# A network's first layer: the next gates issued tile by tile between turning steps, and one value through the gates' function behind each square root

## The chip, the cores and the metric

The kernel runs on one core of a Trainium2 chip. The metric is the device time of one execution in microseconds (us). Engines are named as in the profile: PE is TensorE's matmul, PEld its weight load, DVE is VectorE, ACT is ScalarE, POOL is GpSimd, SP is SyncE, which here only issues transfers (DMAs).

## The reference

The input is a batch of eight images of 56 x 56 pixels with 192 channels. Four layers follow one another, each behind a group normalization, with a residual sum. The change touches the first layer only:

```python
p = silu(x @ p_w.T + p_b);  q = silu(x @ q_w.T + q_b);  v = silu(x @ v_w.T + v_b)   # 192 -> 576
qv = q * v
o1 = toeplitz(qv along each row,    a1)    # a1, a2: 56 taps each way, per channel
o2 = toeplitz(qv along each column, a2)
out = (p * (o1 + o2)) @ o_w.T + o_b        # 576 -> 192
```

Layer 1 is a 3 x 3 outlook attention, layer 2 an 8 x 8 window attention with rotary positions, layer 3 a scan over rows and columns. All arithmetic is float32.

## The kernel before

**Stages of the first layer.** For each image `b` there are five stages `c` = 0 to 4. A stage handles 128 of the 576 channels; the fifth, the tail, has 64. A stage consists of four kinds of work:

- *Gates* (`project`): for four groups `g` of the image's pixels, `q` and `v` are computed, each by six matmul calls into one tile of PSUM (L358), then Silu with bias on ACT (L369) into an SBUF tile `s`. So a group has two PSUM tiles; in the tail it has one, whose two halves are `q` and `v`. The products (`multiply`, L381 on DVE and L387 on POOL) write `q * v` into `qv`, once straight and once transposed.
- *Turning* (`turn_both`, `turn`): PE transposes `qv` in seven steps of 16 transposes each (L414). A step fills one PSUM tile, which DVE copies into `ol` (L419), and after it ACT copies the other half into `or` (L419 too). The tail's steps are those of L433 and L440.
- *Convolution* (`convolve`): 32 matmul calls a step (L457), whose results DVE and ACT copy into `ot` (L477, L475, L468).
- *Post* (`post`, `post_tail`): the gate `p` (L499 or L612, Silu L506 or L618), the way back by transposes (L518 or L627, product on DVE L523 or L632), the output's matmuls (L532, L553, L640, L655), and the addition into the accumulator `acc` on DVE (L484, L486). Post of stages 0 and 1 runs in stage 2, that of 2 and 3 in stage 4, and that of the tail (`post_tail`) in stage 0 of the next image.

**One stage ahead.** In stage `c` the gates of stage `c + 1` are issued. The products of the next stage overwrite `qv`, so they come behind the turning steps. The gates need not: `early` holds the first two of the four groups, which are issued between turning steps, with their products directly behind the turning. The other two run behind that, as wholes.

```python
early = [] if fill else ahead[0:2]
ring["wide"] = c not in (2, 4)
merge(fill + [f for f, _ in early], turns)
```

`fill` is the post work that a stage takes over. It is present in stages 2 and 4, and in stage 0 of every image but the first. So gates go between turning steps in stages 1 and 3, and in stage 0 of image 0. `merge(a, b)` spreads the two lists evenly over each other.

**Buffers.** PSUM tiles come from a ring: three tiles `c` and, as every fourth where `ring["wide"]` holds, one tile `o`. A PE step that takes a tile waits until its earlier contents have been read by the engines that copy or add them. The SBUF tiles `s` are a ring of six.

**Normalization.** The statistics (`bn_stats`, L156 on DVE, twelve for the next image's input `x` and eleven for `acc`) and two small rounds of matmuls (L129) end in a square root on ACT (L170). In stage 0 the statistics of the finished `acc` are told to the next layer (`tell`), `acc` is stored (L71), and the next image's `x` is loaded (`load_raw`, L89, sixteen transfers into one of two buffers). In stage 1 `acc` is loaded anew (L73) and `tell` ends (L693). In stage 2 the next image is normalized (`normalize`, L49 and L680).

**Who orders what.** Only PE's instructions keep the order in which the program issues them (`manual_schedule` names PE alone for this layer). DVE's, ACT's, POOL's and SP's instructions are put into an order by the scheduler when the kernel is built. On the chip each engine then works its queue in that order, and an instruction whose input is not there holds up all behind it. SP has at most eight transfers under way: each one waits for the one eight places before it.

**Function tables.** Where ACT goes from Sqrt to Silu or back, a table load (ACT_TABLE_LOAD) stands in front of the activation.

Of the kernel before, what the change touches and what calls it, by code (L numbers as in the profile page):

```python
# [9 lines left out]
AF = mybir.ActivationFunctionType  # L10
# [37 lines left out]
def affine(eng, out, in_, scale, bias):  # L48
    eng.tensor_scalar(out, in_, scale, bias, ALU.mult, ALU.add)  # L49
# [128 lines left out]
def layer0(cx, xin, xout, w, consts):  # L178
# [6 lines left out]
    tc, nc = cx.tc, cx.nc  # L185
    B = len(xin)
    NS, DS = 9, 64
# [3 lines left out]
    halves = slice(0, CB), slice(CB, 128)  # L191
    cx.open(B)
    cx.between = ExitStack()
    with ExitStack() as es:
        gn = GroupNormSplit(cx, cx.between, w["gmat"], es, w["gmat3"])
# [8 lines left out]
        def banks():  # L204
            if ring["wide"]:
                ring["at"] += 1
                if ring["at"] % 4 == 0:
                    return cx.tile(psc, [128, 2, 512], "o", bufs=1)
            return cx.tile(psc, [128, 2, 512], "c")

        def work(*shape):
            n = int(np.prod(shape))
            t = cx.tile(wk, [128, 4 * 4 * H], "s")[:, 0:n]
            return t.rearrange("p (a b) -> p a b", a=shape[0])
# [10 lines left out]
        wqv, wps = {}, {}  # L225

        def fetch_wqv(q, queue=nc.sync):
            if q < B * NC:
                wqv[q] = cx.tile(cp, [128, 3, 2, 128], "wqv", bufs=2)
                queue.dma_start(wqv[q], w["w_qv"][q % NC])  # L230
# [12 lines left out]
        with ExitStack() as pes:  # L243
# [11 lines left out]
            n = 1  # L255
# [10 lines left out]
            for t in (1, 2):  # L266
# [13 lines left out]
                for i in range(3):  # L280
                    ps = banks()[0:32, 0, 0:NP]
# [4 lines left out]
                for s in range(NS):  # L286
                    ps = banks()[0:DS, 0, 0:NP]
# [54 lines left out]
        def project(xn, q):  # L342


            n = 7 * H
            c = q % NC
            tail = c == NC - 1
            js = [2 * c] if tail else [2 * c, 2 * c + 1]

            state = {}  # L350

            def gates(g):
                pss = []
                for i in range(len(js)):
                    ps = banks()
                    for k in range(3):
                        for h, rows in enumerate(halves):
                            nc.tensor.matmul(  # L358
                                ps[:, h, 0:n], wqv[q][rows, k, i, :],
                                xn[rows, k, g * n : (g + 1) * n],  # L360
                                start=(k == 0), stop=(k == 2),
                            )
                    pss.append(ps)
                ts = []
                for i in range(2):
                    j, ps = js[0 if tail else i], pss[0 if tail else i]
                    rows = slice(i * DS, (i + 1) * DS) if tail else slice(0, 128)
                    t = work(2, n)[0 : DS if tail else 128]
                    nc.scalar.activation(t, ps[rows, :, 0:n], AF.Silu, bias=bqv[rows, j : j + 1])  # L369
                    ts.append(t)  # L370
                state[g] = ts

            def products(g):
                multiply(g, slice(0, DS if tail else 128), state.pop(g))

            return [(lambda g=g: gates(g), lambda g=g: products(g)) for g in range(4)]

        def multiply(g, rows, ts):

            def straight():  # L380
                nc.vector.tensor_tensor(  # L381
                    sub(qv[rows, 7 * g :, 64 + H - 1 :], (HH * 120, 2), (120, 7), (-1, H)),
                    *(t.rearrange("p u (h w) -> p u h w", w=H) for t in ts), ALU.mult,
                )

            def across(eng, u, w0, w1):
                eng.tensor_tensor(  # L387
                    sub(qv[rows, w0:, H - 1 - 7 * g - HH * u :], (120, w1 - w0), (-1, 7)),
                    *(t[:, u].rearrange("p (h w) -> p w h", w=H)[:, w0:w1] for t in ts), ALU.mult,
                )  # L390

            if g < 3:
                straight()
                for u in range(2):
                    across(nc.gpsimd, u, 0, H)
                return

            for i, w in enumerate(((0, HH), (HH, H))):
                across(nc.gpsimd, 0, *w)
                across(nc.vector, 1, *w)  # L400
                if i == 0:
                    straight()
# [193 lines left out]
        def post_tail(xn, ot, acc):  # L596
# [68 lines left out]
            steps = [lambda f=f, g=g: f(g) for f in (back, out) for g in range(2)]  # L665
            return [gates, *steps, lambda: (rest(0), rest(1))]

        def normalize(xn):

            measures, deviate, settle = gn.steps(*((xn[:, k], 4) for k in range(3)))  # L670

            def measure():
                for f in measures:
                    f()

            def last():
                rstd, nbias = settle(banks)
                for k in (0, 2):
                    affine(nc.vector, xn[:, k], xn[:, k], rstd[:, k : k + 1], nbias[:, k : k + 1])
                nc.scalar.activation(  # L680
                    xn[:, 1], xn[:, 1], AF.Identity, bias=nbias[:, 1:2], scale=rstd[:, 1:2]
                )

            return [measure, lambda: deviate(banks), last]

        def tell(b, xa, xb):

            measures, deviate, settle = gn.steps((xa, 7), (xb, 4))

            def last(bank):  # L690
                nn = cx.tile(gn.small, [128, 2, 2], "nn")
                for i, v in enumerate(settle(bank)):
                    nc.vector.tensor_copy(nn[:, :, i], v)  # L693
                nc.sync.dma_start(cx.norms[b][0:CA], nn[:, 0, :])
                nc.sync.dma_start(cx.norms[b][CA:], nn[0:CB, 1, :])

            return measures, [deviate, last]

        def merge(a, b):

            n = max(len(a), len(b))
            for i in range(n):
                for x in (a, b):
                    for f in x[-(-i * len(x) // n) : -(-(i + 1) * len(x) // n)]:
                        f()
# [7 lines left out]
        xn, nxt = first, None  # L713
# [1 line left out]
        for n in range(2):  # L715
            toeplitz(n)
        def whole(steps):
            return [lambda f=f, h=h: (f(), h()) for f, h in steps]

        merge(whole(project(xn, 0)), [])  # L720
        fill, after, telling = [], None, []
        for b in range(B):
            more = b + 1 < B
            for c in range(NC):
                n = b * NS + 2 * c
                two = c < NC - 1
                turns = turn_both(n) if two else turn(n)

                i = b * NC + c
                fetch_wqv(i + 2)  # L730
                ahead = project(xn if two else nxt, i + 1) if two or more else []
                early = [] if fill else ahead[0:2]
                ring["wide"] = c not in (2, 4)
                merge(fill + [f for f, _ in early], turns)
                ring.update(at=0, wide=True)
                for _, f in early:
                    f()
                ahead = whole(ahead[len(early) :])
                if fill:
                    fetch_wp({2: 1, 4: 2, 0: 0}[c])  # L740
                fill, beside = [], []
                if c == 0:
                    if after is not None:
                        image_dma(nc.sync, xout[b - 1], *after, store=True)
                        beside, telling = tell(b - 1, *after)
                    if more:
                        nxt = load_raw(b + 1)
                if c == 1:
                    acc = new_acc(b)
                    beside = [lambda f=f: f(banks) for f in telling]  # L750
                if c == 2 and more:
                    beside = normalize(nxt)

                if c % 2 == 0:
                    ot = cx.tile(cp, [120, H, 128] if two else [H, H, DS], "ot")
                convs = []
                for m in (n, n + 1) if two else (n,):
                    *some, last = convolve(m, ot)
                    convs += some + [lambda m=m, last=last: (last(), toeplitz(m + 2))]

                if c == NC - 2:
                    k = len(ahead)
                    ahead = [f for pair in zip(ahead, convs[0:k]) for f in pair]
                    convs = convs[k:]
                merge(ahead, beside)
                for f in convs:
                    f()
                if c in (1, 3):
                    fill = post(c // 2, xn, ot, acc)
            fill, after = post_tail(xn, ot, acc), acc  # L770
            xn = nxt
# [1448 lines left out]
```

## Time and profile before

| | us |
|---|---|
| median of 3 runs | 4054.93 (4053.79 to 4061.73) |
| the profiled execution | 4069.0, of which the span is 4067.2 |
| PE busy in the span | 3786.1 (93%) |
| DVE / ACT / POOL busy | 2371.5 / 1789.6 / 1523.3 |
| first layer, from the first matmul to the last image's post | about 27 to 1935 |
| image 5, stage 0: from the tail's first post matmul to the first whole gates | 1231.0 to 1250.2 |

The rows read as follows. The page gives each engine's busy time. A row of the timeline gives start, duration, engine, line, operation and tiles, how many instructions are merged in it, and in brackets how long the engine had been idle before it and who ended that. A row of the windows gives, for one stretch, the busy time of PE, PEld, DVE, ACT and POOL with their counts, the granted clock, the DMA engines' share and their GB/s.

### The profile page before, as it was taken

To read this page: it belongs to the slowest core of one execution; us is meant where nothing else is said; L and a number is where in the kernel's file an instruction comes from. 1 tells how busy PE (TensorE), PEld (TensorE's weight loads), DVE (VectorE), ACT (ScalarE), POOL (GpSimd) and SP (SyncE) were. 2 spreads that over 40 slices of the span, in tenths; PEclk is the share of its full clock that TensorE was granted. 3 is DMA by queue.
4 is the path that set the end of the run, shared out by engine and by line. 5 is a ranking of instruction groups with operands and counts; after the bars stand their busy time and mean duration, and the time that the engine had idled before them with its cause. 6 is when DMAs were issued, how large, how long until landed. Compare 5 with 4: busy or idle time off the path is not lost. (4 is left out here: it accounts for less than half of the span.)

```text
span 4067.2 us, 115859 instructions
## 1 busy us (share of the span) xinstructions
PE 3786.1 (93%) x51036; PEld 2655.7 (65%) x51036; DVE 2371.5 (58%) x3318; ACT 1789.6 (44%) x2021; POOL 1523.3 (37%) x1325
## 2 busy tenths in 40 slices
PE   6989999999998999999799999899989999998997
PEld 4777767677776767777566666444435455556997
DVE  6556565655657565555544444565566667665654
ACT  2434444344444434443334433243335555554564
POOL 3222242222233222223433333333334444444776
PEclk9999999999999999999899999999999999999999
DMA  7865353533526352342333443556557766653333
GB/s 158 169 143 131 81 142 103 125 77 98 125 76 160 85 136 72 89 105 76 108 104 103 107 104 94 167 166 209 166 163 184 181 153 154 153 132 102 99 99 98
DMA packets 390300, 507.94 MB, mean 125 GB/s; under 512 B 176932, under 2 KB 326724, under 8 KB 388404
## 3 DMA queue, kind: packets, MB, share of 16 engines
q1 hardware_dynamic: 385621, 494.07, 47.6%
q8 instruction: 401, 6.57, 0.7%
q10 hardware_dynamic: 3135, 3.47, 0.3%
q0 software_dynamic: 1040, 2.99, 0.3%
q14 instruction: 103, 0.84, 0.1%
HBM read 344.69 MB, written 155.65 MB: 123 GB/s over the span
## 5 line engine op out<-in xcount | busy, mean ns | idle before, releaser
L387 POOL TENSOR_TENSOR qv<-s,s 128x392 f32<-128x392 f32 (+3 forms) x320 | 569.3, 1806 | 1296.4 <-ACT s L369 1048.5
L358 PE MATMUL c<-x,wqv 64*128 64x392 f32 x2856 | 518.3, 509 | 45.9 <-ACT or L419 24.7
L358 PEld LDWEIGHTS c<-x,wqv 64*128 64x128 f32 x2856 | 285.0, 193 | 223.6 <-ACT or L419 29.8
L369 ACT ACTIVATE s<-c,bqv 128x784 f32<-128x784 f32 (+1 forms) x270 | 244.9, 913 | 330.0 <-PE c L358 308.1
L381 DVE TENSOR_TENSOR qv<-s,s 128x784 f32<-128x784 f32 (+1 forms) x160 | 229.0, 1441 | 132.0 <-ACT s L369 132.0
L499 PE MATMUL c<-x,wp 64*128 64x224 f32 x2688 | 282.1, 356 | 17.0 <-ACT s L506 14.4
L419 DVE COPY ol<-c 56x1024 f32<-56x1024 f32 x184 | 218.7, 1208 | 113.6 <-PE c L414 113.6
L499 PEld LDWEIGHTS c<-x,wp 64*128 64x128 f32 x2688 | 254.5, 189 | 21.7 <-ACT s L506 16.6
L523 DVE TENSOR_TENSOR s<-s,c 128x896 f32<-128x896 f32 x112 | 121.8, 1088 | 239.6 <-ACT s L506 233.3
L419 ACT COPY or<-c 56x1024 f32<-56x1024 f32 x184 | 184.0, 1008 | 175.8 <-DVE ol L419 169.5
L457 PEld LDWEIGHTS c<-or,ol 120*64 120x64 f32 x7168 | 217.3, 139 | 40.4 <-issue 38.0
L457 PE MATMUL c<-or,ol 120*64 120x56 f32 x7168 | 225.3, 224 | 19.3 <-issue 10.1
L2084 POOL TENSOR_TENSOR y<-y,s 128x448 f32<-128x448 f32 x168 | 185.2, 1102 | 95.8 <-ACT s L2063 95.8
L1552 ACT ACTIVATE vb<-sm 128x1024 f32<-128x1024 f32 (+1 forms) x100 | 103.9, 1040 | 261.1 <-issue 218.2
L2053 PE MATMUL h<-ringv,am 128*64 128x57 f32 (+1 forms) x4400 | 192.7, 235 | 21.8 <-DVE ringv L2040 13.9
L506 ACT ACTIVATE s<-c,bp 128x448 f32<-128x448 f32 x224 | 129.7, 630 | 185.5 <-PE c L499 184.1
L1541 PE MATMUL v<-wvb,wa 128*128 128x512 f32 (+1 forms) x400 | 192.1, 613 | 6.4 <-ACT wa L1427 6.4
L2053 PE MATMUL h<-ringh,am 128*64 128x57 f32 (+1 forms) x4400 | 186.3, 232 | 8.8 <-DVE ringh L2059 8.8
L2053 PEld LDWEIGHTS h<-ringv,am 128*64 128x64 f32 x4400 | 168.1, 140 | 25.4 <-DVE ringv L2040 14.9
L1060 PE MATMUL c<-wv,xc 128*126 128x192 f32 x896 | 175.4, 339 | 0.0
L2053 PEld LDWEIGHTS h<-ringh,am 128*64 128x64 f32 x4400 | 166.3, 139 | 11.1 <-DVE ringh L2059 11.1
L1570 POOL TENSOR_TENSOR l<-vb,ta 128x512 f32<-128x512 f32 (+1 forms) x52 | 75.2, 1446 | 259.5 <-ACT vb L1552 258.5
(268 smaller groups left out, 7708.7 us busy)
## 6 DMA issues: line engine op xcount, KB each, us to landing
or<-tt SPq DMA_DIRECT2D x252, 196.0 KB
ol<-tt SPq DMA_DIRECT2D x252, 196.0 KB
vt<-v SPq DMA_DIRECT2D x56, 672.0 KB
v<-vb SPq DMA_DIRECT2D x96, 384.0 KB
x<-x SPq DMA_DIRECT2D x110, 168.0 KB
wqv<-in_l_w_qv SPq DMA_DIRECT2D x38, 384.0 KB
x<-in_x SPq DMA_DIRECT2D x64, 196.0 KB
x<-x SPq DMA_DIRECT2D x110, 112.0 KB
```

Source lines behind the costliest of these rows:

```text
L358: nc.tensor.matmul(ps[:, h, 0:n], wqv[q][rows, k, i, :], xn[rows, k, g * n : (g + 1) * n], start=(k == 0), stop=(k == 2),)
L369: nc.scalar.activation(t, ps[rows, :, 0:n], AF.Silu, bias=bqv[rows, j : j + 1])
L381: nc.vector.tensor_tensor(sub(qv[rows, 7 * g :, 64 + H - 1 :], (HH * 120, 2), (120, 7), (-1, H)), *(t.rearrange("p u (h w) -> p u h w", w= ...
L387: eng.tensor_tensor(sub(qv[rows, w0:, H - 1 - 7 * g - HH * u :], (120, w1 - w0), (-1, 7)), *(t[:, u].rearrange("p (h w) -> p w h", w=H)[:, ...
L419: copy(dst[:, :, :, i0 : i0 + 8], view[rows])
L457: nc.tensor.matmul(ps[u * 64 : (u + 1) * 64, k, v * H : (v + 1) * H], left[:, d * H : d * H + 64], right[:, d * H : (d + 1) * H], start=Tr ...
L499: nc.tensor.matmul(ps[:, h, u * n : (u + 1) * n], wps[j][rows, k, u, :], xn[rows, k, g * n : (g + 1) * n], start=(u == 0 and k == 0), stop ...
L506: nc.scalar.activation(sp[:, u].rearrange("p (h i) -> p h i", h=2), ps[:, :, u * n : (u + 1) * n], AF.Silu, bias=bp[:, 2 * j + u : 2 * j + ...
L1060: nc.tensor.matmul(out(i, u), group(i, u), wv[0], start=(u == 0), stop=True, skip_group_check=True,)
L1541: nc.tensor.matmul(out, x[:, at : at + n], wt, start=(k == 0), stop=(k == 1), skip_group_check=True,)
L2053: nc.tensor.matmul(ps[sides[c], y], am[a][:, m * CB : (m + 1) * CB], old[:, x], start=(n < 2), stop=True, skip_group_check=True,)
L2084: nc.gpsimd.tensor_tensor(v, v, line[:, j], ALU.add)
```

## The change

Four edits, all in the first layer.

1. `gates(g)`, which issued both PSUM tiles of a group and then both activations, becomes `gate(g, i)` for one tile and its activation. `project` returns for each group a list of such calls and the products.
2. `early` is filled in stages 0, 1 and 3 of every image. So stage 0 of images 1 to 7, the stage that carries the tail's post, gets the first two groups too.
3. The tile calls are first spread over `fill`, and the result over the turning steps. In stage 0 this gives ten pieces (six of post, four gate tiles) over seven turning steps; in stage 1 four gate tiles.
4. `ready()` puts a single value through Silu, into a tile that nothing reads. It is called behind both square roots, in the last image only where a gate follows.

```diff
-            def gates(g):
-                pss = []
-                for i in range(len(js)):
-                    ps = banks()
...
-                    pss.append(ps)
-                ts = []
-                for i in range(2):
-                    j, ps = js[0 if tail else i], pss[0 if tail else i]
-                    rows = slice(i * DS, (i + 1) * DS) if tail else slice(0, 128)
+            def gate(g, i):
+                ps = banks()
...
+                j = js[i]
+                for rows in halves if tail else [slice(0, 128)]:
                     t = work(2, n)[0 : DS if tail else 128]
                     nc.scalar.activation(t, ps[rows, :, 0:n], AF.Silu, bias=bqv[rows, j : j + 1])
-                    ts.append(t)
-                state[g] = ts
+                    state.setdefault(g, []).append(t)
...
-            return [(lambda g=g: gates(g), lambda g=g: products(g)) for g in range(4)]
+            return [
+                ([lambda g=g, i=i: gate(g, i) for i in range(len(js))], lambda g=g: products(g))
+                for g in range(4)
+            ]
...
+        def ready():
+            t = cx.tile(gn.small, [1, 1], "ready")
+            nc.scalar.activation(t, gn.eps[0:1], AF.Silu)
...
                 rstd, nbias = settle(banks)
+                ready()
...
-                for i, v in enumerate(settle(bank)):
+                told = settle(bank)
+                if b + 1 < B:
+                    ready()
+                for i, v in enumerate(told):
...
-            return [lambda f=f, h=h: (f(), h()) for f, h in steps]
+            return [lambda fs=fs, h=h: [f() for f in (*fs, h)] for fs, h in steps]
...
-                early = [] if fill else ahead[0:2]
+                early = ahead[0:2] if c in (0, 1, 3) else []
                 ring["wide"] = c not in (2, 4)
-                merge(fill + [f for f, _ in early], turns)
+                woven = []
+                merge(
+                    [lambda f=f: woven.append(f) for f in fill],
+                    [lambda f=f: woven.append(f) for fs, _ in early for f in fs],
+                )
+                merge(woven, turns)
```

More of the change, by code (lines that the diff above doesn't have):

```diff
@@ L350, in project @@
             state = {}
-            def gates(g):
-                pss = []
-                for i in range(len(js)):
-                    ps = banks()
[L356 to L362, printed above, removed]
-                    pss.append(ps)
-                ts = []
-                for i in range(2):
-                    j, ps = js[0 if tail else i], pss[0 if tail else i]
-                    rows = slice(i * DS, (i + 1) * DS) if tail else slice(0, 128)
+            def gate(g, i):
+                ps = banks()
+                for k in range(3):
+                    for h, rows in enumerate(halves):
+                        nc.tensor.matmul(
+                            ps[:, h, 0:n], wqv[q][rows, k, i, :],
+                            xn[rows, k, g * n : (g + 1) * n],
+                            start=(k == 0), stop=(k == 2),
+                        )
+                j = js[i]
+                for rows in halves if tail else [slice(0, 128)]:
                     t = work(2, n)[0 : DS if tail else 128]
                     nc.scalar.activation(t, ps[rows, :, 0:n], AF.Silu, bias=bqv[rows, j : j + 1])
-                    ts.append(t)
-                state[g] = ts
+                    state.setdefault(g, []).append(t)
             def products(g):
                 multiply(g, slice(0, DS if tail else 128), state.pop(g))
-            return [(lambda g=g: gates(g), lambda g=g: products(g)) for g in range(4)]
+            return [
+                ([lambda g=g, i=i: gate(g, i) for i in range(len(js))], lambda g=g: products(g))
+                for g in range(4)
+            ]
         def multiply(g, rows, ts):
@@ L731, in layer0 @@
                 ahead = project(xn if two else nxt, i + 1) if two or more else []
-                early = [] if fill else ahead[0:2]
+                early = ahead[0:2] if c in (0, 1, 3) else []
                 ring["wide"] = c not in (2, 4)
-                merge(fill + [f for f, _ in early], turns)
+                woven = []
+                merge(
+                    [lambda f=f: woven.append(f) for f in fill],
+                    [lambda f=f: woven.append(f) for fs, _ in early for f in fs],
+                )
+                merge(woven, turns)
                 ring.update(at=0, wide=True)
```

## The prediction, made before the changed kernel ran

> **What bounds the kernel now.** I read the page first: engines, then groups.
>
> ```profile
> span 4067.2 us, 115859 instructions
> ...
> PE 3786.1 (93%) x51036; PEld 2655.7 (65%) x51036; DVE 2371.5 (58%) x3318; ACT 1789.6 (44%) x2021; POOL 1523.3 (37%) x1325
> ...
> L419 DVE COPY ol<-c 56x1024 f32<-56x1024 f32 x184 | 218.7, 1208 | 113.6 <-PE c L414 113.6
> ```
>
> PE is the bound on the whole, so the time is PE's work plus the idle time of PE, and a stretch in the first layer is worth what PE gains or loses in it. Next I cut stage 0 of image 5 into windows: the turning with the tail's post, then the four whole groups of gates, then the convolution.
>
> ```profile
> 1231.00:1250.20 19.20, 14.72 (x226) 9.21 (x222) 16.82 (x25) 8.64 (x9) 0.07 (x1) 1.00 0.79 205
> 1250.20:1266.30 16.10, 16.10 (x96) 9.21 (x96) 16.03 (x28) 8.41 (x9) 9.47 (x6) 1.00 0.90 216
> 1266.30:1276.80 10.50, 7.80 (x258) 7.63 (x256) 7.48 (x11) 1.82 (x2) 3.30 (x3) 1.00 1.02 236
> ```
>
> In the turning window PE works 14.72 of 19.20 us, but DVE works 16.82. In the gates' window PE is full. PE's timeline says where the 4.5 us of idle time are.
>
> ```profile
> 1240.16 0.93 PE L640 MATMUL c<-s,wo 64*128 64x392 f32 x4 [0.77 <-ACT or L419]
> ...
> 1242.18 1.59 PE L640 MATMUL c<-s,wo 64*128 64x392 f32 x8 [0.61 <-ACT or L419]
> ...
> 1245.20 0.89 PE L655 MATMUL o<-s,wo 64*64 64x392 f32 x8 [0.97 <-ACT or L419]
> ...
> 1248.75 0.68 PE L414 MATMUL c<-ident,qv 64*120 64x64 f32 x16 [1.38 <-ACT or L419]
> 1250.17 1.26 PE L358 MATMUL c<-x,wqv 64*128 64x392 f32 x6 [0.74 <-PE c L414]
> ```
>
> Each wait is for a PSUM tile that DVE and, after DVE, ACT must empty ("ACT or L419" starts when DVE's `ol` has ended). Images 1 to 7 show the same five waits (0.77, 0.61, 0.97, 1.38, 0.74). Stage 1 has one, 1.86 us, before its first whole gates. DVE's timeline gives the prices and the order of its queue:
>
> ```profile
> 1238.99 0.95 DVE L632 TENSOR_TENSOR s<-s,o 128x784 f32<-128x784 f32 x1
> ...
> 1241.01 1.97 DVE L486 TENSOR_TENSOR acca<-c,acca 128x392 f32<-128x392 f32 x4
> ...
> 1249.99 2.33 DVE L419 COPY ol<-c 56x1024 f32<-56x1024 f32 x2
> 1252.26 2.71 DVE L156 BATCH_NORM_STATS2 st<-acca 128x6 f32<-128x448 f32 x5
> ...
> 1260.07 1.96 DVE L156 BATCH_NORM_STATS2 st<-x 128x6 f32<-128x392 f32 x4
> ```
>
> The statistics of the next `x` (the last row, st<-x) stand 10 us behind the last turning copy (1249.99 plus 2.33).
>
> **Part 1: gate tiles into stage 0 (images 1 to 7).** Four gate tiles of 2.04 us (24 matmuls in 8.2 us) move from the gates' window into the turning window. On PE alone this would fill the 4.5 us. But DVE's order is the scheduler's, and the program as built shows it. Copies of steps 0 to 6 are t0 to t6, way back is B, two additions to `acc` are "+", statistics of `acc` and `x` are a and x, the straight product is Q, the aggregate is g:
>
> ```
> before: t0 B t1 B t2 + + t3 + a + t4 (accb+) a (accb+) t5 t6 | a a a a a ... x x ...
> after:  t0 t1 B t2 x x x x B t3 + x + t4 Q a a x + a + t5 a a a a x g x x t6 Q (accb+) (accb+) ...
> ```
>
> Nine of the next image's twelve `x` statistics, five more of `acc`'s, and one product now stand in front of the seventh copy, t6. That matters twice. First, the wait: the four x in front of the second B need two halves of `x` that SP issues at 1235.7 to 1239. In the old trace the landing events put the fifth of these transfers (needed by the first x) at 1244.44, 13.4 us into the stage; in images 1 to 6 at 12.6 to 13.5. The seventh, which the third x needs, I put at 14.5, by the 0.5 us between landings. DVE gets there at 10.5: PE gives t0, t1, B, t2 by 8.4, and t2's copy ends at 10.5. So DVE, and behind it the second B, every later copy and addition, stands for 3 us. Second, the work behind the wait, by the distances of the rows above: four x 1.96, B 0.88, four copies (t3 to t6) at 1.16 make 4.64, eight additions at 0.49 make 3.94, five x at 0.49 make 2.45, seven a at 0.54 make 3.79, Q 0.95, g 0.22. Together 18.8, so t6's copy ends at 13.5 + 18.8 = 32.3, and ACT's half at 33.3 (1.01 a copy). The first whole gate tile takes t6's PSUM tile, so PE cannot go on before 33.3. Four gate tiles are left, 8.2: the convolution starts at 41.5. The same walk over the old order gives 35.8 (the trace has 35.3). I take walk against walk: 5.7 us later, in each of images 1 to 6. Nothing takes it back: what follows is PE's own work.
>
> Image 7 loads no next image, so its DVE order has no x. The walk gives 36.0 against 35.8: 0.2.
>
> Bounds: if the x halves were there when DVE comes, t6 still ends at 29.2 and an image loses 2.6. If they land 3 us later than I take, it loses 8.7. For landing I take the old trace's times, since the first five issues are unchanged; the sixth to twelfth now go ahead of the stores, on the same saturated transfers (205 GB/s in that window).
>
> What else moves: SP now issues twelve x loads before the first store instead of five, and the stores of `acc` and the reload wait for later additions. In the old trace the reload has landed by 1278 and is first used at 1328.6 (accb, L484); 10 us later it is still in time. POOL's order is unchanged; its products end 1270.1 in the old trace, and the next turning needs them at 1280.9. Its first product can start once step 6 is transposed, near 26, so it is no later. The `s` ring: the four early gates take tiles whose products were read before the turning began.
>
> **Part 2: tile by tile in stage 1 (and stage 0 of image 0).** PE's 11.7 us of gates and turning are better mixed, but two straight products now stand in DVE's queue before the sixth and seventh copies, and the second waits for the fourth gate tile's Silu. By the same walk PE waits 0.9 and 1.2 before the whole gates instead of 1.86: +0.1 each in eight images, about +1. Stage 3 keeps its order: 0.
>
> **Part 3: `ready`.** As built, all fifteen of them stand at the head of ACT's queue, because nothing ties them to the square roots: one table load and fifteen one-element activations, between the transfer issue that ends at 9.6 and the one at 26.5, where ACT is idle. I cost them at 0; if each took 0.3 us (Sqrt on 128x2 takes 0.30) they end by 16. The load behind each square root stays where it was:
>
> ```profile
> 1312.27 1.28 ACT L506 ACT_TABLE_LOAD   x1 [1.61 <-PE c L499]
> 1313.56 1.16 ACT L506 ACTIVATE s<-c,bp 128x448 f32<-128x448 f32 x2
> ```
> ```profile
> 1314.77 2.54 PE L499 MATMUL c<-x,wp 64*128 64x224 f32 x24 [1.65 <-ACT s L506]
> ```
>
> That load of 1.28 us sits between L499 and its Silu, and PE waits 1.65 for it in each of seven images. This stays.
>
> **Two rules of the Trainium skill.** The rows: a load takes 1.28 us, and the Silu behind it starts 0.01 us after its end; fifteen removed loads would be worth at most 19 us, and none is removed. "ScalarE: Activation LUTs", section "What ACT_TABLE_LOAD costs", adds some 1380 ns of drain to such a load's 1283 ns. By it fifteen removed switches would be worth 40 us; the trace shows no drain here. The second row is DVE's 16.82 busy of 19.20 in the turning window: the evacuation is the long side there, and the gate tiles bring DVE no relief. "Perfetto Trace Analysis", section "Matmuls", has independent matmul groups rotate through PSUM banks so that the evacuation of one overlaps the next group. By that rule alone the four gate tiles would fill PE's idle time, a gain in all seven images.
>
> **Sum.** 6 x 5.7 + 0.2 + 1 = +35 us. The profiled execution, 4069.0 (span 4067.2 and 1.8 around it), becomes 4104. It lies 14 above the median of the runs, so the runs' median should go from 4054.93 to 4090.
>
> **Rivals.**
>
> *DVE keeps up and PE's gaps close (faster).* Place: stage 0. It decides where t6's copy ends before 26 us of the stage instead of 32.3; at its best, PE's own 14.7 + 8.2 = 23 fill the stage and the convolution starts at 31, 4.2 earlier: -30 over seven images, 4025. For it: PE's idle time is real, and the product Q now runs beside an idle POOL at about 0.95 (mean 1.44). Against: 18.8 us of DVE work between 13.5 and t6. Chance 0.08.
>
> *A draw.* The x halves are there early, and PE's waits for "issue" shrink. In images 1 to 6 PE stands 2 to 3.5 us between 40 and 48 us of the stage, the engine waiting for nothing that the profile shows, where the transfers run at 216 to 236 GB/s; image 7, with less traffic, has none. If the new order of transfers thins them there, -2.6 x 6 = -16, which with the lower bound 2.6 x 6 = +16 leaves 4055. Chance 0.06.
>
> *Worse.* Landing 3 us later, or those waits doubled: +35 + 18, 4108, or with both 4124. Chance 0.14.
>
> *`ready` works where it is written.* Then PE's 1.65 in seven images, -12, goes off any of these sums. The order as built speaks against it; under 0.03, and within the range.
>
> **Numbers.** The forecast, 4074 to 4105, has 0.70. The range takes in the bounds of landing (+16 and +54) and half of the "issue" waits: 4062 to 4110. The measurement tells about 0.2%, 8 us. Faster by more: 0.08; within: 0.06; slower: 0.86.
>
> **What would show it.** In the new profile: DVE idle 2 to 4 us before st<-x in stage 0, released by the transfer of x; the last `ol` copy some 32 us into the stage; PE waiting near 4 us for "ACT or" before the first whole gates; about 41 us from the tail's first post matmul to the convolution; L506's table loads still seven. If the stage's first part is 31 us or less to the convolution, or DVE does not wait for x, the forecast is wrong.

## The result, and the profile after

The changed kernel takes 4120.51 us (median of 4 runs, 4109.71 to 4121.96) against 4058.33 for the kernel before (4053.79 to 4064.24, 4 runs): ratio 1.0147, interval 1.0123 to 1.0170. By this ratio it is 60 us slower (the medians differ by 62). The forecast, 4090 with a range to 4110, has the direction and the place and is too low by 31 us. The profiled execution took 4109.7 us, 41 more than that of the kernel before. Three lines of its page:

```profile
span 4107.9 us, 115933 instructions
...
PE 3801.8 (93%) x51036; PEld 2655.8 (65%) x51036; DVE 2348.8 (57%) x3318; ACT 1794.9 (44%) x2037; POOL 1510.5 (37%) x1325
...
L416 DVE COPY ol<-c 56x1024 f32<-56x1024 f32 x183 | 218.8, 1209 | 108.1 <-PE c L411 108.1
```

PE issues the same 51036 matmuls and is busy 15.7 us longer (3786.1 before). DVE's copy costs what it did (1209 ns, before 1208). So of the 41 us only some 25 can be new waiting; in the rest PE does the same work more slowly. Stage 0 of image 5 in windows (start, end, length; busy time and instructions of PE, PEld, DVE, ACT, POOL; then granted clock, DMA share and GB/s):

```profile
1260.68:1279.80 19.12, 14.22 (x192) 9.02 (x188) 11.73 (x15) 9.27 (x10) 0.08 (x1) 0.98 0.80 192
1279.80:1295.40 15.60, 11.18 (x82) 5.91 (x82) 14.73 (x26) 5.04 (x6) 5.72 (x4) 0.80 0.57 168
1295.40:1305.20 9.80, 9.80 (x50) 5.39 (x50) 6.68 (x18) 2.74 (x3) 3.97 (x3) 0.83 0.68 179
1305.20:1315.70 10.50, 9.33 (x268) 8.60 (x268) 5.39 (x5) 2.73 (x3) 3.99 (x3) 1.00 0.98 244
```

The clock column read 1.00 in all three windows before; here it is 0.80 and 0.83 in the middle two. The four whole gate tiles (third line) need 9.80 us instead of 8.2. PE's timeline has the waits that stand ahead of these windows (start, busy time, instruction, in brackets the idle time before it and what ended it):

```profile
1277.88 0.69 PE L411 MATMUL c<-ident,qv 64*120 64x64 f32 x16 [3.67 <-DVE s L629]
1280.04 4.29 PE L356 MATMUL o<-x,wqv 64*128 64x392 f32 x12 [1.48 <-ACT or L416]
...
1295.38 7.89 PE L356 MATMUL c<-x,wqv 64*128 64x392 f32 x36 [3.95 <-ACT or L416]
1303.11 2.14 PE L356 MATMUL o<-x,wqv 64*128 64x392 f32 x12
1305.18 5.11 PE L454 MATMUL c<-or,ol 120*64 120x56 f32 x166
```
```profile
1274.98 1.97 DVE L156 BATCH_NORM_STATS2 st<-x 128x6 f32<-128x392 f32 x4 [3.73 <-DMA x<-in_x]
...
1293.09 1.20 DVE L416 COPY ol<-c 56x1024 f32<-56x1024 f32 x1
```

DVE stands 3.73 us for the transfer of `x`, PE 3.67 us behind DVE, and after that wait twelve gate matmuls take 4.29 us; the same twelve take 2.14 further down. The last `ol` copy starts 32.4 us into the stage, PE then waits 3.95 us, and the next 36 matmuls take 7.89 us where three times 2.14 would be 6.4. The convolution starts 44.5 us into the stage: 35.3 before, 41.5 by the forecast.

**An account of PE's time.** From the start of image 1's stage 0 to the end of image 7's stage 4, PE's time is work at full clock, plus idle time (the sum of all PE waits in the timeline), plus half-speed loss. The trace's clock records are at 1 or at 0.5; half of the time at 0.5 that lies outside of PE's waits is lost. For the kernel before this gives 1624.2 = 1494.8 + 107.5 + 21.9 us; for the changed kernel 1666.6 = 1494.1 + 134.6 + 37.9. In the twelve traces of this study the first term stays between 1489 and 1498 us, so the other two carry every difference:

| kernel | ratio to before (interval) | stretch | idle | half-speed loss |
|---|---|---|---|---|
| before | 1 | 1624.2 | 107.5 | 21.9 |
| changed | 1.0147 (1.0123 to 1.0170) | 1666.6 | 134.6 | 37.9 |
| changed, no `ready` | 1.0137 (1.0115 to 1.0159) | 1678.8 | 137.6 | 46.1 |
| changed, `x` held back | 1.0021 (1.0008 to 1.0035) | 1628.1 | 110.7 | 19.9 |
| changed, without stage 0 | 1.0003 (0.9987 to 1.0020) | 1627.6 | 115.2 | 14.3 |
| changed, DVE in program order | 1.0161 (1.0143 to 1.0179) | 1668.7 | 132.4 | 45.1 |
| the same, and ACT | 1.0129 (1.0111 to 1.0147) | 1660.3 | 123.0 | 45.4 |
| the same, norms' DVE work early | 0.9887 (0.9866 to 0.9907) | 1573.8 | 68.2 | 16.5 |
| the same, no gates in stage 0 | 0.9944 (0.9929 to 0.9959) | 1598.6 | 90.4 | 11.1 |
| before, `ready` tied | 0.9965 (0.9951 to 0.9979) | 1613.1 | 96.3 | 21.2 |
| before, added wait | 1.0092 (1.0065 to 1.0119) | 1654.3 | 128.1 | 29.0 |
| before, longer added wait | 1.0158 (1.0133 to 1.0183) | 1676.9 | 141.9 | 38.6 |

### The profile page after: what moved, and what is told of

Read it like the earlier page. It is cut to its first block, busy times and chain, and to the rows that moved or that the text cites. A ratio compares the mean times of both kernels' runs of the same rounds, so it can differ in the third digit from the quotient of the medians.

```text
span 4107.9 us, 115933 instructions
## 1 busy us (share of the span) xinstructions
PE 3801.8 (93%) x51036; PEld 2655.8 (65%) x51036; DVE 2348.8 (57%) x3318; ACT 1794.9 (44%) x2037; POOL 1510.5 (37%) x1325
## 4 chain that ended last, share of the span: by engine, by line
PE 69%; DVE 10%; issue 7%; ACT 6%; DMA 4%; POOL 2%; SPq 2%; DVEq 0%; POOLq 0%; ACTq 0%
PE c L356 9%; PE h L2063 7%; PE v L1551 6%; PE c L496 5%; PE c L454 4%; PE c L1070 4%; PE o L529 4%; PE y L1105 3%; PE kv L1611 3%; PE o L356 2%; DVE ol L416 2%; PE c L1076 2%; ACT or L416 2%; PE c L550 2%; PE c L1773 2%
## 5 line engine op out<-in xcount | busy, mean ns | idle before, releaser
L384 POOL TENSOR_TENSOR qv<-s,s 128x392 f32<-128x392 f32 (+3 forms) x320 | 555.7, 1763 | 1355.2 <-ACT s L364 922.3
L378 DVE TENSOR_TENSOR qv<-s,s 128x784 f32<-128x784 f32 (+1 forms) x160 | 218.0, 1366 | 155.2 <-ACT s L364 155.2
L416 DVE COPY ol<-c 56x1024 f32<-56x1024 f32 x183 | 218.8, 1209 | 108.1 <-PE c L411 108.1
L496 PEld LDWEIGHTS c<-x,wp 64*128 64x128 f32 x2688 | 251.6, 187 | 21.7 <-ACT s L503 16.7
L503 ACT ACTIVATE s<-c,bp 128x448 f32<-128x448 f32 x224 | 129.7, 630 | 182.2 <-PE c L496 180.9
L529 PE MATMUL o<-s,wo 64*128 64x224 f32 x1536 | 170.6, 359 | 0.0
```

The costliest lines, as they stand in the source:

```text
L378: nc.vector.tensor_tensor(sub(qv[rows, 7 * g :, 64 + H - 1 :], (HH * 120, 2), (120, 7), (-1, H)), *(t.rearrange("p u (h w) -> p u h w", w= ...
L384: eng.tensor_tensor(sub(qv[rows, w0:, H - 1 - 7 * g - HH * u :], (120, w1 - w0), (-1, 7)), *(t[:, u].rearrange("p (h w) -> p w h", w=H)[:, ...
L416: copy(dst[:, :, :, i0 : i0 + 8], view[rows])
L496: nc.tensor.matmul(ps[:, h, u * n : (u + 1) * n], wps[j][rows, k, u, :], xn[rows, k, g * n : (g + 1) * n], start=(u == 0 and k == 0), stop ...
L529: nc.tensor.matmul(outs[q][:, h, i * n : (i + 1) * n], wo[rows, 2 * j + u, 0:CA], gated[g][rows, u, h * n : (h + 1) * n], start=(i == 0 an ...
```

## Experiments

The theory: the loss is made in stage 0, by DVE's order (its wait for `x`, and statistics ahead of the seventh copy), and PE's longer waits cost half-speed clock on top. The rivals: the interleaving itself costs, `ready` carries a part, stage 1 carries a part, or a wait costs its length alone.

**Without `ready`.**

```diff
-        def ready():
-            t = cx.tile(gn.small, [1, 1], "ready")
-            nc.scalar.activation(t, gn.eps[0:1], AF.Silu)
...
-                ready()
```

> The changed kernel without `ready` (the function and its two calls). Theory: the fifteen one-element activations ran in an idle stretch of ACT at the head of its queue and nothing else of theirs remains, so the time is that of the changed kernel, 4120 within 8 us, and stage 0 of images 1 to 6 is still 43.6 to 45.3 us to its convolution. Rival (`ready` moved the order of ACT or of the other engines and so carries a part of the loss): the time comes back by 12 us or more, and the waits in the first layer differ from the changed kernel's.

Median 4126.93 beside a kernel before at 4072.21, ratio 1.0137 against 1.0147: the loss is whole without it. `ready` did nothing that these runs can tell.

**Tile by tile without stage 0.**

```diff
-                early = ahead[0:2] if c in (0, 1, 3) else []
+                early = [] if fill else ahead[0:2]
```

> The changed kernel without its stage 0: early gate tiles go into stages 1 and 3 (and stage 0 of image 0) alone, as in the kernel before, but tile by tile; `ready` stays. Theory (the loss is stage 0's): stage 0's convolution at 35.3 to 37 us as before, stage 1's wait of 1.86 us becomes two of 0.7 and 1.84, +0.7 in eight images, so 0 to +10 against the kernel before. Rival (weaving tile by tile costs in stage 1 as well, by DVE's products ahead of the copies or by half-speed clock behind two waits): +15 to +30.

Ratio 1.0003, that is -5 to +8 us. Stage 0's convolution is back at 35.3 to 36.9 us. What tile by tile costs in stage 1 is too small to tell here; the loss is stage 0's.

**The next `x` held back.** A copy of six columns of `accb`, written by the tail's last additions, goes into `x` ahead of its load.

```diff
+            if behind is not None:
+                seen = behind[:, HQ - 6 :].rearrange("p (a b) -> p a b", a=3)
+                nc.vector.tensor_copy(x[:, :, 0 : HQ : HQ // 2], seen)
...
-                        nxt = load_raw(b + 1)
+                        nxt = load_raw(b + 1, after[1] if after else None)
```

> The changed kernel with the next image's load of `x` tied behind the tail's post in images 1 to 6: a small DVE copy from the added `accb` into `x` stands before the load, so no statistics of `x` can be put between the turning copies. Theory (DVE's wait for the transfer and the statistics put ahead of the seventh copy delay the whole gates): no DVE wait for `x` in stage 0; its convolution comes at 36 to 40 us, as in image 7, instead of 44.4; 6 images give -25 to -50, that is 4070 to 4095, and the granted clock's half-speed time falls. The load now comes later and could delay the norm of the next image in stage 1: that would show as a PE wait there and take up to 15 us of it back. Rival (the gate tiles among the turning steps cost by the PSUM ring or by PE's own order, wherever DVE's statistics lie): the convolution stays at 43 to 45 us and the time at 4115 to 4125.

Median 4078.31, 49 us less than the kernel without `ready` that ran beside it (4126.93). The gate tiles are all still there, and the ratio is 1.0021, so the interleaving, with what else DVE's queue puts ahead of the copies, costs some 9 us (3 to 14) of the 55. Its PE and DVE timelines in stage 0 of image 5 (which starts at 1239.96):

```profile
1268.49 7.59 PE L359 MATMUL c<-x,wqv 64*128 64x392 f32 x36 [4.06 <-ACT or L419]
1275.92 2.14 PE L359 MATMUL o<-x,wqv 64*128 64x392 f32 x12
1277.99 4.23 PE L457 MATMUL c<-or,ol 120*64 120x56 f32 x137
```
```profile
1266.19 1.21 DVE L419 COPY ol<-c 56x1024 f32<-56x1024 f32 x1
```

No DVE wait for `x` is left ahead of the copies, the last `ol` copy starts at 26.2 us instead of 32.4, the convolution at 38.0 (38.6 on average over images 1 to 6, beside 44.4 with the change and 35.8 before). So two thirds of the delay go with `x`. One PE wait of 4.06 us stays, as in image 7, and 7.59 us for 36 matmuls behind it. So even without `x` in the way DVE is the late engine, and the gain that the change could have here does not come.

**DVE, then ACT too, in program order.**

```diff
-        es.enter_context(tc.manual_schedule(engines={mybir.EngineType.PE}))
+        es.enter_context(tc.manual_schedule(engines={mybir.EngineType.PE, mybir.EngineType.DVE}))
```

> The changed kernel with DVE, like PE, in the order in which the program writes its instructions in the first layer; nothing else is changed. Theory (the loss is DVE's queue order, not the gate tiles): the seventh copy follows its turning step at once, PE's 14.7 us of turning and 8.2 us of gate tiles fill stage 0, the convolution comes at 31 to 34 us instead of 44.4 in images 1 to 6 and 39.5 in image 7, and stage 1's waits fall under 0.7 us: against the changed kernel -60 to -90, so 4030 to 4060, at or under the kernel before. Rival A (PE's waits go, but the statistics, now behind, are late for the norm of stage 1 or for the next image): the convolution of stage 0 comes early and a new PE wait of 3 us or more stands in stages 1 to 3; 4060 to 4120. Rival B (the cost is in the interleaving itself): stage 0 stays over 40 us and the time over 4100.

> As the kernel with DVE in program order, with ACT in program order too, so that each `ready` stands behind its square root. Theory: the table load goes out of the way of the post's Silu, PE's 1.65 us at the first Silu after the post go in seven images, so some 12 us less than the kernel with DVE alone in program order. Rival (the load is only moved, the Sqrt table's load or ACT's order makes another wait of the same size, or ACT in program order delays the gates' Silu): within 5 us of that kernel, or slower.

With DVE in program order the convolution starts at 32.1 us in all seven images: the gate tiles fill stage 0 as the theory says. But the time is 4134.58, worse than rival A allowed. Stage 1 has got a wait of 4.57 us in images 1 to 7, and stage 2 one of 5.86 in images 1 to 6. Half-speed loss in stage 0 is gone, and 45.1 us of it stand behind those waits and elsewhere. The second, in image 5:

```profile
1414.05 3.15 PE L129 MATMUL c<-mean,gmat 64*128 64x1 f32 x28 [5.85 <-DVE mean L161]
1417.03 3.65 PE L356 MATMUL c<-x,wqv 64*128 64x392 f32 x10
```
```profile
1406.20 5.71 DVE L156 BATCH_NORM_STATS2 st<-x 128x6 f32<-128x392 f32 x12
...
1413.21 0.49 DVE L160 BATCH_NORM_AGGREGATE mv<-st 128x2 f32<-128x24 f32 x3
```

The twelve statistics now run in one piece where the program writes them, and the norm's small matmul waits for the aggregate behind them; ten gate matmuls after it take 3.65 us. The mean clock is 0.970, the lowest of all kernels. With ACT in program order as well the time is 4122.59, 12.0 less: the 1.65 us wait that ends at L503 is gone in seven images (11.6), as expected; idle time in the table falls by 9.4.

**The third part alone, tied to the square root** (on the kernel before):

```diff
+        def ready(v):
+            t = cx.tile(gn.small, [1, 1], "ready")
+            nc.scalar.activation(t, v[0:1, 0:1], AF.Silu)
...
+                ready(rstd)
```

> The kernel before with a `ready` that reads the reciprocal behind each square root instead of the constant, so that it cannot stand at the head of ACT's queue; no gate tile is moved. Theory (the third part of the change, done so that it works, takes the 1.28 us table load out of the way of the post's first Silu): PE's wait of 1.65 us there goes in seven images, -12, and a little more or less by the clock: -8 to -20 against the kernel before. Rival (the load is hidden elsewhere or the wait only gets another cause): within 5 us of the kernel before.

Ratio 0.9965, so 14 us faster (9 to 20). ACT's timeline:

```profile
1295.55 1.28 ACT L670 ACT_TABLE_LOAD   x1
1299.25 0.20 ACT L670 ACTIVATE ready<-rstd 1x1 f32<-1x1 f32 x1 [2.42 <-DVE rstd L171]
...
1304.00 1.16 ACT L506 ACTIVATE s<-c,bp 128x448 f32<-128x448 f32 x2 [1.62 <-PE c L499]
```

The Silu table's load of 1.28 us now runs 8 us ahead of the post's first Silu. In the changed kernel it still stands before it:

```profile
1349.95 1.28 ACT L503 ACT_TABLE_LOAD   x1 [1.60 <-PE c L496]
```

Seven waits of 1.65 us less are 11.6; idle time fell by 11.2 and the half-speed loss by only 0.7. These seven waits cost close to their length.

**A wait put into the kernel before**, in stage 2 of each image between the gates and the convolution; the longer one has the loop, the other not:

```diff
+            ps = banks()
+            for k in range(3):
+                nc.scalar.activation(ps[:, :, 0:392], held["t"], AF.Silu)
+            nc.scalar.activation(holds, ps[:, 0, 0:128], AF.Silu)
+            nc.tensor.matmul(
+                ps[:, 0, 0:1], holds[0:64, 0:128], holds[0:64, 0:1], start=True, stop=True
+            )
```

> The kernel before with one artificial wait of PE in stage 2 of each of the eight images, between the last whole gate tile and the convolution: a one-column matmul that reads what ACT made of that gate tile (its Silu of 0.91 us and one more of 128 columns). By the rows PE should wait 1.2 to 1.8 us in each image. Theory (a PE wait costs its own length, and over some 2 to 3 us of length it costs half-speed clock on top): a short wait, so close to its length, +10 to +15, and perhaps some half-speed clock in a part of the images, up to +25. Rival (a wait costs its length alone): +10 to +15.

> As the kernel with the short artificial wait, with three Silu of 784 columns (0.91 us each) ahead of it, so that PE waits 2.7 us longer in each of eight images: 4 to 4.6 us. Theory (clock): after each wait of this length the granted clock goes to one half for 3.4 to 10 us, as behind the 3.95 us wait of the changed kernel, so each image loses 4.3 plus 1.7 to 5 us: +48 to +75 against the kernel before, and the run's mean clock falls by 0.005 or more. Rival (length alone): 2.7 x 8 = 22 over the short wait, +32 to +37 in all, at an unchanged clock.

I sized both waits wrongly: ACT has the norm's activation (1.69 us), a table load (1.28) and two gate Silus in front, as its timeline in the longer case shows:

```profile
1416.23 1.69 ACT L693 ACTIVATE x<-x,nbias,rstd 128x1568 f32<-128x1568 f32 x1 [2.45 <-DVE nbias L172]
1417.94 1.28 ACT L369 ACT_TABLE_LOAD   x1
1419.23 1.72 ACT L369 ACTIVATE s<-c,bqv 128x784 f32<-128x784 f32 x2
```

So PE waits 4.46 and 7.00 us, and only where a norm stands beside it; image 7 has 1.36 and 3.90. The short wait so was not short, and cannot show what I wanted of it; the tied `ready` shows it instead. Its cost, 37 us (26 to 48), holds the length alone (7 x 4.46 + 1.36 = 33). The longer one costs 64 (54 to 74), and length alone would be 7 x 7.00 + 3.90 = 53, just outside; the clock shows more than the times do. Its PE timeline, and the windows behind the wait:

```profile
1423.89 0.58 PE L677 MATMUL c<-hold 64*128 64x1 f32 x2 [7.00 <-ACT hold L676]
1424.40 3.67 PE L458 MATMUL o<-or,ol 120*64 120x56 f32 x64
```
```profile
1423.80:1427.20 3.40, 3.31 (x54) 3.29 (x56) 0.41 (x1) 0.04 (x1) 0.03 (x1) 0.50 0.00 0
1427.20:1430.60 3.40, 3.40 (x88) 3.40 (x86) 1.09 (x1) 0.00 (x0) 0.00 (x0) 0.68 0.37 109
1430.60:1434.00 3.40, 3.40 (x124) 3.40 (x120) 1.09 (x1) 0.91 (x1) 0.00 (x0) 1.00 0.63 175
```

The clock is 0.50, then 0.68, then 1.00. 64 convolution matmuls take 3.67 us, 57 ns each; at full clock it is 31 ns (5.11 us for 166 in the changed kernel's timeline above). Only ACT's work, PE's wait for it, a one-column matmul and a PSUM tile of the ring for it were put in, and the kernel before has no half-speed stretch at this place in images 1 to 6, so here the wait is the cause. Directly behind the seven longer waits stand 2.6 us of half-speed loss each, behind the seven of 4.46 us 2.9 each. Not all of it is new loss: in the whole table it grew by 16.7 us (2.4 a wait) and 7.1 (1.0 a wait), because other stretches went. By the times, what exceeds the length is 1.6 us a wait (0.2 to 3.1) and 0.7 (-0.9 to 2.3).

**The change with DVE's order mended.** To the kernel with DVE and ACT in program order: the statistics of the next `x` go into stage 1's convolution, the aggregates ahead of the matmuls that read them, the stored image's first norm matmuls among stage 1's gate tiles. And the same without gate tiles in stage 0.

```diff
+                if c == 1 and telling:
+                    telling[0].gather()
+                    woven.insert(2, lambda: telling[0](banks))
                 merge(woven, turns)
...
-                for f in convs:
-                    f()
+                merge(convs, parts if c == 1 and more else [])
```

> The kernel with DVE and ACT in program order, with the norms' DVE work written earlier: the next image's twelve statistics of `x` in stage 1's convolution instead of in one piece in stage 2, both aggregates ahead of the matmuls that read them, and the first matmuls of the stored image's norm among stage 1's gate tiles. Theory (what the program order lost was its two new waits, 4.57 us in stage 1 and 5.86 us in stage 2 of each image, with the clock behind them): both waits fall under 1 us, 10.4 us in seven images is -70, and the clock rises: 4025 to 4060, faster than the kernel before by 10 to 45 us. Rival (the statistics take another place in DVE's full queue and delay the copies there): new PE waits of 1 to 4 us in stage 1's convolution or turning, and 4070 to 4110.

> The kernel with DVE and ACT in program order and the norms' work early, without the gate tiles in stage 0 of images 1 to 7; all else stays. Theory (with DVE kept to the order in which PE needs it, the gate tiles do fill PE's idle time in stage 0, which is what the change is about): the convolution comes at 35 to 37 us instead of 32.1, seven images give +20 to +35 against the kernel with them, 4035 to 4055 beside a kernel before at 4055 to 4075. Rival (DVE's order did it all, and the gate tiles are worth nothing): within 6 us of the kernel with them, near 4017.

The first takes 4017.53 us, ratio 0.9887: 46 us under the kernel before, and under every other kernel here. Neither of the two waits is left; smaller ones of 1.5 to 4.2 us have come some 75 us into an image, at the end of the second convolution and in the post behind it, in images 1 to 6. Its stage 0 of image 5, from the tail's post to the convolution, in one window:

```profile
1208.25:1240.30 32.05, 30.25 (x320) 18.38 (x316) 24.44 (x31) 17.05 (x18) 10.44 (x7) 1.00 0.78 208
```

PE is busy 30.25 of 32.05 us at full clock, with DVE at 24.44. Without the gate tiles in stage 0 the convolution starts at 34.3 us, under the 35 to 37 expected, and the ratio is 0.9944. The difference of the ratios, 0.0057, is 23 us (13 to 33); idle time differs by 22.2. So the tiles are worth some 23 us once DVE serves PE in its order. Stage 0 shows 15 of it (2.2 us in seven images); the rest is idle time behind the convolution, 4.5 us of it one wait in image 1, and that it comes of the tiles is not shown. Of the 46 us, some 14 can be `ready`'s, as the tied one on the kernel before has it.

## Why the prediction was right and wrong

**DVE's queue in stage 0: right.** The new order puts a wait and the statistics ahead of the seventh copy, in images 1 to 6. In image 5 the wait is 3.73 us (forecast 3; 2.4 to 4.5 over the six images), the seventh copy ends at 33.6 us (32.3), PE's wait for it is 3.95 (near 4), its first whole gates start at 34.7 (33.3). Holding `x` back takes two thirds of the delay away, and DVE in program order all of it.

**The price of the stage: too small, and this is the step that failed.** "Four gate tiles are left, 8.2: the convolution starts at 41.5" priced PE's waits by their length and everything behind them at full clock; the sum has no term for half-speed work and gives no reason for that. Over seven images, idle time in stage 0 up to the convolution went from 31.3 to 60.9 us (+29.6; the forecast's 34.4 was close), but half-speed loss there went from 3.2 to 31.2 (+28.1; forecast nothing). In the kernel without `ready` it is 29.3. An image's convolution is 8.6 us later on average (44.4 against 35.8, images 1 to 6), 4.7 of it idle. Behind the convolution the "issue" waits gave back 8.2 us (16.0 to 7.8), which the forecast saw only in the draw.

**Image 7: 0.2 forecast, some 4 measured.** By the walk the first whole gates start at 27.8 us (36.0 less 8.2); they start at 28.5. The gates then take 11.0 us, not 8.2, behind a wait of 4.05. It has no `x` and no DVE wait, and the walk gave it next to no loss: of its 4.2 us, 1.2 are idle time and 2.9 half-speed loss.

**The step from the profiled execution to the median: it did not hold.** I took off 14 us because the profiled run of before lay 14 above its median. The profiled run of the changed kernel lies 11 below its own. By the profiled pair alone the change is +41, near the forecast's +35; by the ratio of the runs it is +60. That the profiled pair comes near is luck. A kernel's runs differ with their clocks: the changed kernel's took 4109.7, 4119.2, 4121.9 and 4122.0 us at 0.977, 0.976, 0.975 and 0.974, and the profiled one is the fastest of them. Elsewhere than in stage 0's first part its trace has 12 us less half-speed loss than that of before (6.6 against 18.7); the kernel without `ready` has 2 less (16.8), and its stretch is 55 us longer, as its median says. Why the profiled run of before lay high stays open: other runs of that kernel at the same clock, 0.981, took 4062 to 4074.

**Part 2 (+1): small, as forecast, but not by its sum.** Stage 1's waits are 0.72 and 1.84 instead of 1.86, so +0.7 in each image and not +0.1 (the forecast's own 0.9 and 1.2 already make +0.2); over eight images that is less than the run without stage 0 can tell (-5 to +8 us).

**Part 3 (0): right.** As a rival `ready` in its place was put at -12; tied to the square root it gives -14 (-9 to -20). Seven PE waits of 1.65 us make 11.6 of that, so the drain that the Trainium skill ("ScalarE: Activation LUTs", section "What ACT_TABLE_LOAD costs") adds to a load is not seen here either: in ACT's timeline above, the load of 1.28 us stands 0.02 us behind one activation and 0.01 us ahead of the next.

**The rivals.** "DVE keeps up" did not come, and needed another order of DVE's queue to come: then the convolution starts at 32.1 us, against the 31 put for it, and the rule of the Trainium skill ("Perfetto Trace Analysis", section "Matmuls") holds there, with some 23 us. "Worse" had the size (4108 to 4124) by another cause.

## What to carry to other kernels

Work that fills an engine's waits is only worth them if the engine that ends the waits is not made later: look at its queue as built, at what the scheduler puts ahead of the one instruction that is waited for. Where PE is the bound, price a PE wait of 3 us or more at its length plus 1 to 3 us for the half-speed work behind it: 2.6 to 2.9 stood directly behind the added waits, 1.0 to 2.4 net of what went elsewhere. An instruction that is to stand behind another in a scheduled queue must read something of it, or the scheduler moves it away.

## What the runs showed of the hardware

The clock's dependence on PE's waits was sharper than I had thought. In the twelve traces, from image 1's stage 0 to the end of image 7, every stretch at 0.5 begins within a PE wait of 1.2 us or more, or up to 3.5 us after it. Of 67 waits of 3.8 us and over, all 67 have one; their mean length is 4.9 us behind waits under 4.1, 6.7 up to 5, and 9.1 above. Of 9 waits of 3 to 3.8 us 8 have one. Of 265 waits of 1.2 to 3 us 89 do, mostly of one step of 3.4 us, and only three of the 89 share theirs with a longer wait: short waits are not free of it. The Trainium skill, "TensorE: Matmul & The Clock Gate", section "HAM oscillation — how this bites in real kernels", asks for no PE idle gap over about 3.4 us; the long waits agree with it. The same page, section "What's actually happening", puts the ramp's price under 1% of a typical kernel. Here half-speed loss is 1.3% of the table's stretch in the kernel before (21.9 of 1624.2 us) and 2.3% in the changed one (37.9 of 1666.6), and about half of what the change costs in stage 0: +28 us beside +29.6 of idle time.
